# A graph network on one core: attention heads in TensorE's columns, and layer 2's edges in chunks of 128 as they lie

## The chip, the cores and the metric

The kernel runs on one core of one Trainium2 chip, as one program. The metric is the time of one execution on the device in microseconds (us); the median of ten runs is given. TensorE is PE in the profile, VectorE is DVE, ScalarE is ACT, GpSimd is POOL, SyncE is SP; PEld is TensorE's loading of weights.

## What is computed

Four layers act on 3125 nodes of 256 features and 100,000 edges, sorted by their target. Each layer is a graph part, a mixing part and a mixture of experts. The change touches the graph parts of layer 2 and layer 3. In short:

```python
# layer 2: the edges' messages, some of them dropped, summed at the target
h = x @ W_pruned.T
norm = |h[src]| * |edge_weight|            # compared with a tenth of its mean
keep = (norm >= 0.1 * mean) | locked[dst] | (src == dst)
agg = segment_sum(edge_weight * keep * h[src], dst)
x = x + agg + b                            # the mixing part is added too

# layer 3: graph attention with 4 heads of 64 features; each node has an edge to itself as well
e = leaky_relu(a_src[src] + a_dst[dst], 0.2)
a = softmax of e over the edges into each dst
x = x + relu(sum over edges of a * h[src])
```

`locked` marks the nodes that a list of 1000 node numbers names.

## The kernel before

**Names.** P = 125 nodes make a block and there are NB = 25 blocks; PIECES are 7 pieces of 500 nodes (the last has 125). `self.x` holds the nodes' features, `self.xt` the normalised features turned (features in partitions). `self.bank()` hands out one of four PSUM banks named `ps`. `evac` copies out of PSUM on DVE and ACT in turn. `arrive(i)` counts the parts that have finished for a piece and starts the norm of the next step when all are there; `together` runs two generators side by side, each yielding the share of it that is done.

**How the order comes about.** The program is written as straight Python; when it is built, each engine gets a fixed order of its instructions. The semaphores between the engines are added then. Nothing is reordered while it runs.

**Preparation** (`prep`). The edges are packed into records of two words (target x 4096 + source, weight) and stored in DRAM as `rec_d`, in the order of the input. `ROOM[b]` is the number of chunks of 128 edges that is reserved for block b; they sum to NC2 = 841. `idx2` holds where each block's edges start.

**Layer 1's experts** (`l1_ffn`). Eight experts run one after the other over 7 pieces: two matmuls with an activation on ACT (L1411, L1416), then one whose result DVE adds into `self.x` (L1422). Layer 2's preparation `l2_prepare` is a generator that is advanced twice from here, once ahead of expert 0 and once after expert 1. Its first part gathers the records by 25 indirect DMAs (`rec_b`, L1445), a block's chunks beside one another. Its second part finds the locked nodes (L1464), spreads them over 128 partitions as `lock` (25 matmuls L1471, copies L1473), and takes the records apart into `idx` (source), `rel` (target less the block's first node), `wgt`, `awt` and `same`.

**Layer 2's graph part** (`l2_gnn`). A head computes column norms (14 squares with sums, L1503), prunes the weights, and writes h with its norm to DRAM as `hx_d`. Then, block by block and in groups of up to 8 chunks: one gather for each chunk of 128 edges (`hg`, L1551, on POOL); `keep` (L1555, L1556); then for each chunk DVE builds a matrix of edges by the block's nodes (L1560), multiplies it by the larger of `lock` and `keep` (L1562), and PE adds its product with `hg` to the block's sum (L1564). Layer 2's mixing part runs beside it.

**Layer 3's graph part** (`l3_gnn_mix`, `l3_dense`). Attention is computed densely: a matrix of edge counts `ctt_d` (sources by targets) lies in DRAM. For two pieces of targets at a time (1000 columns, four groups in all), the targets' factors `rows` are made by matmuls with a repeated column (L1878) and exponentials (L1880). Then for two heads at a time and each block of sources: `cs` is loaded on SP's queue, ACT makes `t5` (L1899), DVE makes `z` (L1902), and PE multiplies `xr`, the sources' 64 features and a column of ones, with `z` into one PSUM bank for each head and piece (L1905). The 65th row of each result is the sum by which the others are divided. After 25 blocks the banks are copied out, turned by transposes (L1920, L1929) and finished on DVE. Layer 3's mixing part runs beside it.

Of the kernel before, what the change touches and what calls it, by code (L numbers as in the profile page):

```python
# [12 lines left out]
F32 = mybir.dt.float32  # L13
I32 = mybir.dt.int32
# [3 lines left out]
AF = mybir.ActivationFunctionType  # L18
OP = mybir.AluOpType
AX = mybir.AxisListType  # L20
PSUM = bass.MemoryType.PSUM
# [45 lines left out]
ROOM = [_room(b * P, b * P + P) for b in range(NB)]  # L67
NC2 = sum(ROOM)

# [19 lines left out]
class Net:  # L89
    NE, TS = 16, 384  # L90

    def __init__(self, tc, a, ctx):
# [14 lines left out]
        self.iota_f = c.tile([128, 128], F32, name="iota_f")  # L107
        nc.gpsimd.iota(self.iota_f, pattern=[[1, 128]], base=0, channel_multiplier=0,
# [171 lines left out]
    def prep(self):  # L280

        nc, a = self.nc, self.a
        self.rec_d = self.dram.tile([1, 2 * EP], F32, name="rec_d")
# [3 lines left out]
        self.idx2 = self.c.tile([128, NB], I32, name="idx2")  # L287
        nc.vector.memset(self.viol, 0.0)
        nc.scalar.dma_start(self.tab, nc.inline_tensor(_tables(), name="windows").ap())
        room = np.stack([np.broadcast_to(np.array(ROOM) * 128.0, (128, NB)),  # L290
                         np.arange(128)[:, None] * 2.0 * np.array(ROOM)], 1).astype(np.float32)
        with ExitStack() as s:
# [3 lines left out]
            nc.scalar.dma_start(rm, nc.inline_tensor(room, name="room").ap())  # L296
# [72 lines left out]
            nc.vector.tensor_sub(gap2, sr[:, 1:], sr[:, :NB])  # L369
            nc.vector.tensor_tensor(gap2, gap2, rm[:, 0, :], op=OP.is_gt)  # L370
            nc.vector.tensor_reduce(self.viol[:, 2:3], gap2, axis=AX.X, op=OP.add)
            i2 = sb.tile([128, NB], F32, name="i2")
            nc.vector.scalar_tensor_tensor(i2, sr[:, :NB], 2.0, rm[:, 1, :], op0=OP.mult, op1=OP.add)
            nc.vector.tensor_scalar(self.idx2, i2, float(2 * EP - 1024), None, op0=OP.min)
# [983 lines left out]
    def l1_ffn(self, before, after):  # L1358
# [4 lines left out]
        with ExitStack() as s:  # L1363
# [25 lines left out]
            def last(i, w):  # L1389
                self.norm_turn_piece(i, w)  # L1390

                x = self.x[:, i // P:(i + w) // P]
                nc.vector.tensor_add(x, x, self.e2["bias"][:P, None, :].to_broadcast([P, w // P, D]))

# [37 lines left out]
    def l2_prepare(self, sb, wk):  # L1432
# [4 lines left out]
        e["w"] = self.load_w(sb, "L2_gnn_W")  # L1437
        li = wk.tile([P, LOCKS // P], I32, name="li", bufs=1)
# [3 lines left out]
        rec = wk.tile([128, NC2, 2], F32, name="rec_b", bufs=1)  # L1442
        c0 = np.cumsum([0] + ROOM).tolist()
        for b in range(NB):
            nc.gpsimd.indirect_dma_start(  # L1445
                out=rec[:, c0[b]:c0[b + 1]].rearrange("p c t -> p (c t)"), out_offset=None, in_=self.rec_d,
                in_offset=bass.IndirectOffsetOnAxis(ap=self.idx2[:, b:b + 1], axis=1))
# [17 lines left out]
        locked = sb.tile([P, NB], F32, name="locked")  # L1465
        nc.vector.tensor_scalar(locked, ps[:P, :NB], 0.0, None, op0=OP.is_gt)

        lock = sb.tile([128, NB, P], F32, name="lock")
# [5 lines left out]
        pk = rec.bitcast(I32)[:, :, 0]  # L1474
        idx = sb.tile([128, NC2], I32, name="idx")
        rel = sb.tile([128, NC2], F32, name="rel_b")
        nc.vector.tensor_scalar(idx, pk, 4095, None, op0=OP.bitwise_and)
        nc.vector.tensor_scalar(idx, idx, N - 1, None, op0=OP.min)
        dI = wk.tile([128, NC2], I32, name="dI", bufs=1)
        nc.vector.tensor_scalar(dI, pk, 12, None, op0=OP.arith_shift_right)  # L1480
        same = sb.tile([128, NC2], F32, name="same")
        nc.vector.tensor_tensor(same, idx, dI, op=OP.is_equal)
        for b in range(NB):
            nc.vector.tensor_scalar(rel[:, c0[b]:c0[b + 1]], dI[:, c0[b]:c0[b + 1]], float(-P * b), None, op0=OP.add)
        wgt = sb.tile([128, NC2], F32, name="wgt")
        nc.vector.tensor_copy(wgt, rec[:, :, 1])
        awt = sb.tile([128, NC2], F32, name="awt")
        nc.vector.scalar_tensor_tensor(awt, wgt, -1.0, wgt, op0=OP.mult, op1=OP.max)
        e.update(lock=lock, idx=idx, rel=rel, same=same, wgt=wgt, awt=awt, c0=c0)
        yield  # L1490

    def l2_gnn(self, sb, wk, pa):
        nc, tc, a = self.nc, self.tc, self.a
        hx = self.dram.tile([N, D + 1], F32, name="hx_d")
        w, lock, idx, rel, same, wgt, awt, c0 = (
            self.e2[k] for k in ("w", "lock", "idx", "rel", "same", "wgt", "awt", "c0"))

        ss = sb.tile([128, HB], F32, name="ss")
        sp = sb.tile([128, HB, len(PIECES)], F32, name="sp")
        for k, (i, n) in enumerate(PIECES):  # L1500
            for h in range(HB):
                sq = wk.tile([128, PW], F32, name="sq", bufs=1)
                nc.scalar.activation(sq[:, :n], self.xt[:, h, i:i + n], AF.Square, accum_out=sp[:, h, k:k + 1])  # L1503
# [41 lines left out]
        for b in range(NB):  # L1545
            ps = pa.tile([P, D], F32, name="acc")
            for c in range(c0[b], c0[b + 1], CPG):
                m = min(CPG, c0[b + 1] - c)
                hg = wk.tile([128, CPG, D + 1], F32, name="hg", bufs=4)
                for j in range(m):  # L1550
                    nc.gpsimd.indirect_dma_start(  # L1551
                        out=hg[:, j, :], out_offset=None, in_=hx,
                        in_offset=bass.IndirectOffsetOnAxis(ap=idx[:, c + j:c + j + 1], axis=0))
                keep = wk.tile([128, CPG], F32, name="keep")
                nc.vector.tensor_mul(keep[:, :m], hg[:, :m, D], awt[:, c:c + m])  # L1555
                nc.vector.scalar_tensor_tensor(keep[:, :m], keep[:, :m], lim, same[:, c:c + m],  # L1556
                                               op0=OP.is_ge, op1=OP.max)
                for j in range(m):
                    to = wk.tile([128, P], F32, name="to", bufs=16)
                    nc.vector.tensor_scalar(to, self.iota_f[:, :P], rel[:, c + j:c + j + 1],  # L1560
                                            wgt[:, c + j:c + j + 1], op0=OP.is_equal, op1=OP.mult)
                    nc.vector.scalar_tensor_tensor(to, lock[:, b, :], keep[:, j:j + 1], to,  # L1562
                                                   op0=OP.max, op1=OP.mult)
                    nc.tensor.matmul(ps, to, hg[:, j, :D], start=(c + j == c0[b]), stop=(c + j == c0[b + 1] - 1))  # L1564
                yield 0.05 + 0.95 * (c + m) / NC2
            nc.vector.tensor_add(self.x[:, b, :], self.x[:, b, :], ps)
            if b % 4 == 3 or b == NB - 1:
                self.arrive(b // 4 * PW)

    def l2_gnn_mix(self):  # L1570
        with ExitStack() as s:
            ms = s.enter_context(self.pool("m2_sb"))
            mw = s.enter_context(self.pool("m2_wk", 2))
            sb = s.enter_context(self.pool("g2_sb"))
            wk = s.enter_context(self.pool("g2_wk", 2))
            pa = s.enter_context(self.pool("g2_ps", 2, space=PSUM))
            mix = self.l2_mix_by_pieces(ms, mw)
            next(mix)
            self.expect(2, self.norm_turn_mean)
            self.together([self.l2_gnn(sb, wk, pa), mix])  # L1580
# [201 lines left out]
    def l3_gnn_mix(self, before, arrivals):  # L1782
# [6 lines left out]
        with ExitStack() as s:  # L1789
# [12 lines left out]
            xr = sb.tile([P, NB, 4, 65], F32, name="xr")  # L1802
            nc.gpsimd.memset(xr[:, :, :, 64:65], 1.0)
            al = sb.tile([P, NB, 8], F32, name="al")
            for b in range(NB):
                ps = self.bank()
                self.mm_tok(ps[:P, :264], self.xt, b, wx)
                nc.vector.tensor_copy(xr[:, b, :, :64], ps[:P, :D].rearrange("p (h d) -> p h d", h=4))
# [22 lines left out]

            us = sb.tile([P, 3, NB, 4], F32, name="us")
# [5 lines left out]
            self.together([self.l3_dense(sb, wk, pa, wx, xr, us, bias), mix], (1.0, 1.15))  # L1838
# [11 lines left out]
    def l3_dense(self, sb, wk, pa, wx, xr, us, bias):  # L1850
# [5 lines left out]
        at = free[:65, 8 * PW:12 * PW].rearrange("p (h d) -> p h d", h=2)  # L1856

        def finish(b, h0, nh, acc):

            nc.vector.tensor_scalar(few[:, b, h0:h0 + nh], acc[:, :, 64], 1e-20, None, op0=OP.is_lt)  # L1860
            rd = wk.tile([P, 4], F32, name="rd")
            nc.vector.tensor_scalar(rd[:, :nh], acc[:, :, 64], 1e-20, None, op0=OP.max)
            nc.vector.reciprocal(rd[:, :nh], rd[:, :nh])
            t = wk.tile([P, 4, 64], F32, name="tf")
            nc.vector.tensor_mul(t[:, :nh], acc[:, :, :64], rd[:, :nh, None].to_broadcast([P, nh, 64]))
            v = self.x[:, b, h0 * 64:(h0 + nh) * 64]
            nc.vector.scalar_tensor_tensor(v, t[:, :nh].rearrange("p h d -> p (h d)"), 0.0, v,
                                           op0=OP.max, op1=OP.add)

        done, there = 0, []  # L1870
        for p0 in range(0, len(PIECES), 2):
            pcs = PIECES[p0:p0 + 2]
            n = sum(w for _, w in pcs)
            for h in range(4):
                for k, (i, w) in enumerate(pcs):
                    ps = self.bank()
                    for c in range(HB):
                        nc.tensor.matmul(ps[:P, :w], wx[:, c, 260 + h:261 + h].to_broadcast([128, P]),  # L1878
                                         self.xt[:, c, i:i + w], start=(c == 0), stop=(c == HB - 1))
# [478 lines left out]
```

## Time and profile before

| | us |
|---|---|
| median of 10 runs | 4825.16 (4818.94 to 4833.33) |
| the profiled execution's own time | 4822.59 |
| its span, first to last instruction | 4820.8 |
| PE busy | 3788.2 (79% of the span) |
| DVE busy | 2452.4 (51%) |
| ACT busy | 1322.5 (27%) |
| POOL busy | 1122.2 (23%) |
| mean granted TensorE clock | 0.86 |
| layer 1's experts 2 to 7 | 1830 to 2233 |
| head of layer 2's graph part | 2233 to 2275 |
| layer 2's edges, first gather to last | 2275.7 to 3356.0 |
| layer 3's dense attention, first `t5` to last matmul | 3644.4 to 4549.5 |

A line of a group gives the source line, the engine and the operation, what it writes and reads, shapes and count, then the busy time, the mean length of one in ns, and the idle time of the engine just before such instructions with what ended it. Busy times count overlapping instructions once. A matmul of float32 operands shows as two records of PE, each with a weight load of its own. In a line of the timeline the first number is the start, the second the length, both in us; what stands in brackets is the engine's idle time before it and what ended that.

### The profile page before, as it was taken

To read this page: it belongs to the slowest core of one execution; us is meant where nothing else is said; L and a number is where in the kernel's file an instruction comes from. 1 tells how busy PE (TensorE), PEld (TensorE's weight loads), DVE (VectorE), ACT (ScalarE), POOL (GpSimd) and SP (SyncE) were. 2 spreads that over 40 slices of the span, in tenths; PEclk is the share of its full clock that TensorE was granted. 3 is DMA by queue.
4 is the path that set the end of the run, shared out by engine and by line. 5 is a ranking of instruction groups with operands and counts; after the bars stand their busy time and mean duration, and the time that the engine had idled before them with its cause. 6 is when DMAs were issued, how large, how long until landed. Compare 5 with 4: busy or idle time off the path is not lost. (4 is left out here: it accounts for less than half of the span.)

```text
span 4820.8 us, 49604 instructions
## 1 busy us (share of the span) xinstructions
PE 3788.2 (79%) x16425; PEld 2514.3 (52%) x16425; DVE 2452.4 (51%) x7872; ACT 1322.5 (27%) x2364; POOL 1122.2 (23%) x1124
## 2 busy tenths in 40 slices
PE   1886895799748799998565556665699999999798
PEld 0675894466534556555444444444464444444465
DVE  6886335454476421115444444555265666667544
ACT  1476100111123223333000000000155655466521
POOL 2000002200143100000777777776000000000011
PEclk8686996799868699999777777777799999999699
DMA  6245611433231000001333333334201112111232
GB/s 179 63 118 139 145 34 37 128 119 118 82 81 25 25 7 14 14 7 44 101 103 104 103 103 103 104 101 116 88 7 37 49 47 55 44 47 52 59 121 65
DMA packets 256290, 360.32 MB, mean 75 GB/s; under 512 B 62959, under 2 KB 199096, under 8 KB 256027
## 3 DMA queue, kind: packets, MB, share of 16 engines
q1 hardware_dynamic: 132514, 168.96, 12.1%
q0 software_dynamic: 66480, 135.56, 10.5%
q10 hardware_dynamic: 57033, 52.54, 3.9%
q8 instruction: 135, 2.21, 0.2%
q14 instruction: 128, 1.05, 0.1%
HBM read 270.31 MB, written 94.92 MB: 76 GB/s over the span
## 5 line engine op out<-in xcount | busy, mean ns | idle before, releaser
L1564 PE MATMUL acc<-hg,to 128*125 128x256 f32 x1682 | 587.4, 516 | 422.3 <-DVE to L1562 399.7
L1551 POOL DMA_INDIRECT hg<-hx_d,idx x841 | 825.2, 981 | 298.1 <-issue 250.0
L1564 PEld LDWEIGHTS acc<-hg,to 128*125 128x125 f32 x1682 | 430.5, 265 | 565.9 <-DVE to L1562 472.8
L1905 PE MATMUL acc<-z,xr 125*65 125x500 f32 (+1 forms) x1400 | 575.0, 553 | 10.4 <-DVE z L1902 8.8
L1902 DVE SCALAR_TENSOR_TENSOR z<-t,us,cs 125x1000 f32<-125x1000 f32 (+1 forms) x400 | 410.1, 1029 | 136.6 <-PE acc L1905 102.9
L1899 ACT ACTIVATE t<-xn,us 125x1000 f32<-125x1000 f32 (+1 forms) x400 | 409.4, 1037 | 237.6 <-DVE z L1902 233.0
L1905 PEld LDWEIGHTS acc<-z,xr 125*65 125x65 f32 x1400 | 188.3, 144 | 313.6 <-issue 269.6
L1422 DVE SCALAR_TENSOR_TENSOR x<-ps,lg,x 125x256 f32<-125x256 f32 x200 | 93.8, 483 | 412.2 <-PE ps L233 412.2
L1555 DVE TENSOR_TENSOR keep<-hg,awt 128x8 f32<-128x8 f32 (+6 forms) x117 | 19.4, 166 | 549.7 <-DMA hg<-hx_d,idx 424.2
L239 PE MATMUL ps<-xt,w 128*128 128x500 f32 (+1 forms) x672 | 270.3, 549 | 9.0 <-DVE x L1422 7.2
L1560 DVE TENSOR_SCALAR to<-iota_f,rel_b,wgt 128x125 f32<-128x125 f32 x841 | 270.6, 362 | 1.3 <-PE acc L1564 0.6
L1562 DVE SCALAR_TENSOR_TENSOR to<-lock,keep,to 128x125 f32<-128x125 f32 x841 | 252.1, 343 | 0.0
L2188 POOL DMA_INDIRECT bx_d<-row,slot x25 | 31.4, 1256 | 925.5 <-ACT t L1899 809.3
L571 PE MATMUL ps<-y,cb 125*125 125x256 bf16 x1875 | 215.5, 280 | 0.0
L571 PEld LDWEIGHTS <-cb 125*125 125x125 bf16 x1875 | 214.3, 141 | 0.1
L779 ACT ACTIVATE k<-k 125x128 f32<-125x128 f32 x50 | 15.8, 315 | 720.5 <-DVE k L778 677.6
L168 ACT ACTIVATE rstd_t<-rstd_t 125x4 f32<-125x4 f32 (+2 forms) x86 | 17.3, 204 | 671.7 <-DVE rstd_t L167 560.9
L233 PE MATMUL ps<-wo,h 128*125 128x256 f32 x800 | 187.7, 386 | 3.6 <-ACT h L1416 2.6
L239 PEld LDWEIGHTS ps<-xt,w 128*128 128x128 f32 x672 | 123.3, 194 | 122.8 <-issue 109.0
L239 PE MATMUL ps<-h,w 128*128 128x500 f32 (+1 forms) x448 | 178.2, 540 | 1.3 <-ACT h L1411 1.3
L239 PE MATMUL pl<-xbt,w 128*128 128x384 f32 x416 | 172.1, 563 | 8.2 <-DVE xbt L1135 5.8
L233 PEld LDWEIGHTS ps<-wo,h 128*125 128x125 f32 x800 | 142.7, 187 | 66.1 <-ACT h L1416 43.7
(558 smaller groups left out, 6288.5 us busy)
## 6 DMA issues: line engine op xcount, KB each, us to landing
cs<-ctt_d SPq DMA_DIRECT2D x150, 218.8 KB
w<-in_L_ffn_w_dram SPq DMA_DIRECT2D x52, 512.0 KB
cnt_d<-cd SPq DMA_DIRECT2D x25, 683.6 KB
cb<-cnt_d SPq DMA_DIRECT2D x25, 683.6 KB
ctt_d<-ct ACTq DMA_DIRECT2D x6, 2734.4 KB
hg<-hx_d,idx POOLq DMA_INDIRECT x841, 2.8
b0x_d<-zero SPq DMA_DIRECT2D x1, 9984.0 KB
xb<-b0x_d SPq DMA_DIRECT2D x26, 384.0 KB
```

What stands on the lines that cost most here:

```text
L233: self.nc.tensor.matmul(ps, xt[:, h, b * P:(b + 1) * P], w[:, h, :], start=(h == 0), stop=(h == k - 1))
L239: self.nc.tensor.matmul(ps, w[:, h, :], xt[:, h, i:i + n], start=(h == 0), stop=(h == k - 1))
L571: nc.tensor.matmul(ps[:P, :D], cf[k][:, h * P:(h + 1) * P], y3[:, b0 + k, j, :], start=(k == 0 and j == 0), stop=(k == m - 1 and j == 2))
L1422: nc.vector.scalar_tensor_tensor(self.x[:, b, :], ps[:P, :D], g[:, b, e:e + 1], self.x[:, b, :], op0=OP.mult, op1=OP.add)
L1551: nc.gpsimd.indirect_dma_start(out=hg[:, j, :], out_offset=None, in_=hx, in_offset=bass.IndirectOffsetOnAxis(ap=idx[:, c + j:c + j + 1], a ...
L1560: nc.vector.tensor_scalar(to, self.iota_f[:, :P], rel[:, c + j:c + j + 1], wgt[:, c + j:c + j + 1], op0=OP.is_equal, op1=OP.mult)
L1562: nc.vector.scalar_tensor_tensor(to, lock[:, b, :], keep[:, j:j + 1], to, op0=OP.max, op1=OP.mult)
L1564: nc.tensor.matmul(ps, to, hg[:, j, :D], start=(c + j == c0[b]), stop=(c + j == c0[b + 1] - 1))
L1899: nc.scalar.activation(t[:, :n], rows[:, k4, :n], AF.Relu, bias=us[:, 2, b, k4:k4 + 1], scale=us[:, 0, b, k4:k4 + 1])
L1902: nc.vector.scalar_tensor_tensor(z[:, :n], t[:, :n], us[:, 1, b, k4:k4 + 1], c, op0=OP.add, op1=OP.mult)
L1905: nc.tensor.matmul(acc[h, k][:, :w], xr[:, b, k4, :], z[:, k * PW:k * PW + w], start=(b == 0), stop=(b == NB - 1))
L2188: st = nc.gpsimd.indirect_dma_start(out=bx, out_offset=bass.IndirectOffsetOnAxis(ap=slot[:, j:j + 1], axis=0), in_=row[:, j, :], in_offset ...
```

## The change

Two edits are made at once.

**Layer 2's edges.** The chunks are no longer reserved block by block: chunk c is edges 128c to 128c + 127 as they lie in the input, 782 in all. `_spans` says at build time which block, or which two blocks, a chunk can fall into (239 of the 782 have two); a deviation from it sets a flag that leads to the general path. `idx2` and the 25 gathers of `rec_b` go; the records are loaded by two plain DMAs with 128 edges along a partition, taken apart, and turned by 21 transposes. The look-up whether an edge's target is locked moves out of the edge loop into `l2_prepare`: for each chunk one DVE operation with an accumulator writes a column of `lk`. In the edge loop the weight is folded into `kw` for a group of 8 chunks, so that one DVE operation makes the matrix (125 or 250 columns), and PE adds it to one block's sum or to two. The squares of the head move to where a piece of `xt` is finished, in layer 1.

**Layer 3's heads.** `xr` loses its column of ones. The matmuls of two heads go to columns 0 to 63 and 64 to 127 of TensorE (`tile_position`) and write one bank; the sums come from further matmuls with 32 columns of ones, each to 32 columns of TensorE, into a third bank. The targets' factors are computed once from `al`, written to DRAM (`r_d`) and loaded spread over the partitions by `target_rows`. `finish` works on 128 rows at a time.

```diff
-ROOM = [_room(b * P, b * P + P) for b in range(NB)]
-NC2 = sum(ROOM)
+NC2 = -(-E // 128)
+def _starts():
+    q = np.sqrt(np.arange(NB) * P / N)
+    return E * q, 4.5 * np.sqrt(E * q * (1 - q)) + 2
+def _spans():
+    at, off = _starts()
+    out = []
+    for c in range(NC2):
+        bs = [b for b in range(NB) if at[b] - off[b] < 128 * c + 128
+              and (b == NB - 1 or at[b + 1] + off[b + 1] > 128 * c)]
+        out.append((bs[0], len(bs)))
+    return out
...
 def l2_prepare(self, sb, wk):
...
-        for b in range(NB):
-            nc.gpsimd.indirect_dma_start(
-                out=rec[:, c0[b]:c0[b + 1]].rearrange("p c t -> p (c t)"), out_offset=None, in_=self.rec_d,
-                in_offset=bass.IndirectOffsetOnAxis(ap=self.idx2[:, b:b + 1], axis=1))
+        nt = -(-NC2 // 128)
+        rec = wk.tile([128, nt, 128, 2], F32, name="rec_b", bufs=1)
+        nc.gpsimd.memset(rec[:, nt - 1], 0.0)
+        flat = self.as_come_d[:, :2 * 128 * NC2].rearrange("o (c t) -> (o c) t", t=256)
+        m = NC2 - 128 * (nt - 1)
+        nc.sync.dma_start(rec[:, :nt - 1].rearrange("p k e t -> p k (e t)"),
+                          flat[:128 * (nt - 1)].rearrange("(k p) t -> p k t", p=128))
+        nc.sync.dma_start(rec[:m, nt - 1].rearrange("p e t -> p (e t)"), flat[128 * (nt - 1):])
         yield
...
+        for out, op, k in ((fr, OP.bitwise_and, 4095), (to, OP.arith_shift_right, 12), (wgt, None, None)):
+            if op is not None:
+                nc.vector.tensor_scalar(part, pk, k, None, op0=op)
+                nc.vector.tensor_copy(whole, part)
+            for t0 in range(0, nt, 4):
+                ps = self.bank()
+                n = min(NC2 - 128 * t0, 512)
+                for t in range(t0, min(nt, t0 + 4)):
+                    nc.tensor.transpose(ps[:, (t - t0) * 128:(t - t0 + 1) * 128],
+                                        rec[:, t, :, 1] if op is None else whole[:, t], self.ident)
+                nc.vector.tensor_copy(out[:, 128 * t0:128 * t0 + n], ps[:, :n])
...
+        lk = sb.tile([128, NC2], F32, name="lk")
+        for c, (b, m) in enumerate(SPANS):
+            junk = wk.tile([128, 2 * P], F32, name="junk")
+            nc.vector.scalar_tensor_tensor(junk[:, :m * P], self.iota_w[:, :m * P], rel[:, c:c + 1],
+                                           lock[:, b:b + m].rearrange("p b n -> p (b n)"), op0=OP.is_equal,
+                                           op1=OP.mult, accum_out=lk[:, c:c + 1])
+        nc.vector.tensor_tensor(to, fr, to, op=OP.is_equal)
+        nc.vector.tensor_tensor(lk, lk, to, op=OP.max)
         yield
...
 def l2_gnn(self, sb, wk, pa):
...
+        for c0 in range(0, NC2, CPG):
+            m = min(CPG, NC2 - c0)
+            hg = wk.tile([128, CPG, D + 1], F32, name="hg", bufs=4)
+            for j in range(m):
+                nc.gpsimd.indirect_dma_start(
+                    out=hg[:, j, :], out_offset=None, in_=hx,
+                    in_offset=bass.IndirectOffsetOnAxis(ap=idx[:, c0 + j:c0 + j + 1], axis=0))
+            kw = wk.tile([128, CPG], F32, name="kw")
+            nc.vector.tensor_mul(kw[:, :m], hg[:, :m, D], awt[:, c0:c0 + m])
+            nc.vector.scalar_tensor_tensor(kw[:, :m], kw[:, :m], lim, lk[:, c0:c0 + m], op0=OP.is_ge, op1=OP.max)
+            nc.vector.tensor_mul(kw[:, :m], kw[:, :m], wgt[:, c0:c0 + m])
+            for j in range(m):
+                c = c0 + j
+                b, nb = SPANS[c]
+                to = wk.tile([128, nb * P], F32, name=f"to{nb}", bufs=10 if nb == 1 else 6)
+                nc.vector.tensor_scalar(to, self.iota_w[:, :nb * P], rel[:, c:c + 1], kw[:, j:j + 1],
+                                        op0=OP.is_equal, op1=OP.mult)
+                for k in range(b, b + nb):
+                    if c == first[k]:
+                        acc[k] = pa.tile([P, D], F32, name="acc")
+                    nc.tensor.matmul(acc[k], to[:, (k - b) * P:(k - b + 1) * P], hg[:, j, :D],
+                                     start=(c == first[k]), stop=(c == last[k]))
+                    if c == last[k]:
+                        nc.vector.tensor_add(self.x[:, k, :], self.x[:, k, :], acc.pop(k))
...
 def l3_gnn_mix(self, before, arrivals):
...
+            r = sb.tile([P, 4, NB], F32, name="r3")
+            for h in range(4):
+                nc.scalar.activation(r[:, h], al[:, :, 4 + h], AF.Exp, bias=bias[:, h:h + 1], scale=0.8)
+            ps = self.bank()
+            nc.tensor.transpose(ps[:4 * NB, :P], r.rearrange("p h b -> p (h b)"), self.ident[:P, :P])
+            rt = sb.tile([4 * NB, P], F32, name="rt3")
+            nc.vector.tensor_copy(rt, ps[:4 * NB, :P])
+            r_d = self.dram.tile([4, N], F32, name="r3_d")
+            nc.sync.dma_start(r_d.rearrange("h (b p) -> (h b) p", p=P), rt)
...
 def l3_dense(self, sb, wk, pa, xr, us, r_d):
...
+        def target_rows(g, h0):
+            if g < len(groups):
+                i, n = groups[g][0][0], sum(w for _, w in groups[g])
+                for h in (h0, h0 + 1):
+                    self.move(nc.sync, rows[:P, h, :n], r_d[h, i:i + n].partition_broadcast(P))
...
                 for b in range(NB):
...
-                        z = wk.tile([P, 2 * PW], F32, name="z", bufs=3)
+                        z = zs[h] = wk.tile([P, 2 * PW], F32, name="z", bufs=4)
...
-                            nc.tensor.matmul(acc[h, k][:, :w], xr[:, b, k4, :], z[:, k * PW:k * PW + w],
-                                             start=(b == 0), stop=(b == NB - 1))
+                    for u, (h0, k, w) in enumerate(units):
+                        for j in range(2):
+                            nc.tensor.matmul(acc[u][64 * j:64 * j + 64, :w], xr[:, b, h0 + j, :],
+                                             zs[h0 + j][:, k * PW:k * PW + w], start=(b == 0), stop=(b == NB - 1),
+                                             tile_position=(0, 64 * j))
+                    for u, (h0, k, w) in enumerate(units):
+                        for j in range(2):
+                            q = 32 * (2 * u + j)
+                            nc.tensor.matmul(acc[2][q:q + 32, :w], self.ones[:P, :32],
+                                             zs[h0 + j][:, k * PW:k * PW + w], start=(b == 0), stop=(b == NB - 1),
+                                             tile_position=(0, q))
...
+                for h0 in hs:
+                    target_rows(g + 1, h0)
+                finish(b0, pcs[0][1] // P, hs[0], 2 * len(hs), acc)
```

## Prediction

> **What bounds the kernel now.** I read the busy times by stage first, then the costliest groups, then the order of single instructions at the three places that the change touches. Columns of the first view: stretch in us, its length, busy time of PE, weight loads, DVE, ACT and POOL with instruction counts, the granted clock, DMA share, GB/s.
>
> ```profile
> 1830.00:2233.00 403.00, 399.32 (x1320) 232.69 (x1318) 99.92 (x245) 126.47 (x183) 0.00 (x0) 1.00 0.03 8
> 2275.00:3360.00 1085.00, 653.99 (x2038) 495.28 (x2036) 516.35 (x2066) 17.93 (x64) 825.22 (x841) 0.77 0.38 103
> 3640.00:4550.00 910.00, 881.21 (x2754) 405.54 (x2752) 604.61 (x1295) 535.80 (x666) 30.20 (x24) 0.97 0.17 47
> ```
>
> Three stages matter. In layer 1's experts (experts 2 to 7 are the first row) PE is busy 399 of 403 us, DVE 100. In layer 2's edges PE and DVE are half idle. In layer 3's dense attention PE is busy 97%. The groups say what paces each:
>
> ```profile
> L1564 PE MATMUL acc<-hg,to 128*125 128x256 f32 x1682 | 587.4, 516 | 422.3 <-DVE to L1562 399.7
> L1551 POOL DMA_INDIRECT hg<-hx_d,idx x841 | 825.2, 981 | 298.1 <-issue 250.0
> ...
> L1905 PE MATMUL acc<-z,xr 125*65 125x500 f32 (+1 forms) x1400 | 575.0, 553 | 10.4 <-DVE z L1902 8.8
> ...
> L1560 DVE TENSOR_SCALAR to<-iota_f,rel_b,wgt 128x125 f32<-128x125 f32 x841 | 270.6, 362 | 1.3 <-PE acc L1564 0.6
> L1562 DVE SCALAR_TENSOR_TENSOR to<-lock,keep,to 128x125 f32<-128x125 f32 x841 | 252.1, 343 | 0.0
> ```
>
> In the edge stage PE waits for DVE's `to`, and behind it DVE's first use of a group waits for `hg` (L1555, 549.7 us): POOL runs its 841 gathers with only issue time between them, so the **gathers pace the stage**, one per (825.2 + 250.0) / 841 = 1.278 us. In the dense stage the 1400 records of L1905 are 700 matmuls, each two records one after the other, 575.0 / 1400 = 0.41 us a record.
>
> The last view is the order of instructions around `l2_prepare`:
>
> ```profile
> 1685.36 0.60 DVE L1477 TENSOR_SCALAR idx<-rec_b 128x841 int32<-128x841 int32 x1 [12.90 <-DMA rec_b<-rec_d,idx]
> ...
> 1690.61 1.04 DVE L1488 SCALAR_TENSOR_TENSOR awt<-wgt 128x841 f32<-128x841 f32 x1
> ```
> ```profile
> 1821.02 8.57 PE L1471 MATMUL ps<-ident,locked 125*128 125x125 f32 x50 [0.28 <-DVE locked L1466]
> 1829.42 3.52 PE L239 MATMUL ps<-xt,w 128*128 128x500 f32 x8
> ```
> ```profile
> 2234.88 1.10 DVE L1560 TENSOR_SCALAR to<-iota_f,rel_b,wgt 128x125 f32<-128x125 f32 x4
> 2235.90 0.15 DVE L169 RECIPROCAL ln_rs<-rstd_t 125x1 f32<-125x1 f32 x1
> 2235.97 0.33 DVE L1560 TENSOR_SCALAR to<-iota_f,rel_b,wgt 128x125 f32<-128x125 f32 x1
> 2236.22 0.41 DVE L187 TENSOR_SCALAR xn<-x,ln_mv,ln_rs 125x256 f32<-125x256 f32 x1
> ```
>
> Two things are to be seen. An engine's order prefers what stands earlier in the program: L1560, late in the program, fills DVE's gaps, and the earlier norm (L169, L187) takes the engine whenever it is ready. And what stands earlier goes first though nobody needs it yet: PE runs all 50 records of L1471, whose result is used 460 us later, ahead of expert 2 (L239).
>
> **Layer 2, gathers.** 841 chunks become 782 (100,000 edges by 128, rounded up), so 59 gathers go: 59 x 1.278 = **-75**. Of the 782, 239 cover two blocks by the rule in `_spans`, so PE gets 1021 matmuls for 841: 360 more records at 587.4 / 1682 = 0.349 us, 126 us. I cost them at nothing: the stage has 1085 - 654 = 431 us of idle PE; without that cover they cost 126. DVE loses L1562 (252 us) and its L1560 grows by 239 wide forms; that is off the path while POOL paces, as are the 60 more small ones of `kw` (98 groups of three for 117 of two).
>
> **Layer 2, edge records.** 25 gathers of `rec_b` become two plain loads on SP, ahead of the first expert weights. DVE's 12.9 us wait goes, and with it PE's 7.2 us behind it (L239 waiting for L1422). Against it stand 0 to 4.5 us by which the loads hold up the weights (782 KB at 179 GB/s, the busiest slice of the page); I take 2: **-5**. The 14 Square pairs move into the last expert's pieces, where ACT is idle two thirds of the time (10 us if that cover is gone). The stage head now waits until 2242.34 for the last pair; the last `xt` copy ends at 2237.9 and one pair takes 1.0, so **-3** (0 to -5.2, PE's whole wait there).
>
> **Layer 2, the lock lookup.** This is the large added term. 782 operations with an accumulator (`lk`) are put into `l2_prepare`, between experts 1 and 2. No row has this form; L1562 is nearest, 252.1 / 841 = 0.300 us each back to back. Width adds (1256 - 348) / 875 = 1.04 ns an element by the two shapes of L1902, so a two-block one is 0.430. The accumulator read adds between 0 and the 0.083 of L327's; I take 0.04, since L327's pairs start 0.98 apart at a length of 1.03. So 543 x 0.34 + 239 x 0.47 = 297 us (266 to 331). They need `lock` (copies from 1821.8 on) and, through 21 new transposes and their copies, `rel`; the block starts between 1822 and 1838, say 1830. By the order just shown they stand ahead of expert 2's L1422 on DVE. Queued behind them are the four L1422 of the first piece, and these hold the four `ps` banks, so PE, which began the second piece at 1839.9, stands until 1830 + 297 + 0.5 = 2127: **+288** (249 to 340). The small precedent is DVE's block at 1685 to 1691.6, during which PE stood 7.2 us for L1422.
>
> **Layer 3.** L1878 goes: 112 records, 48.0 us on the bound engine, **-48**; its exponentials (L1880) were on ACT, off the path. 100 narrow transposes of 65 rows become 75 of 128: 17.4 us against 75 x 7.7 / 50 = 11.6 by L1320's row, **-5**. The start now goes through DRAM, a write and a broadcast read at some 2.8 us each (the landing time of `hg`), while PE has the other branch: +2 (0 to 6). The seven later reloads of target rows wait on SP for ACT's last use; `cs` loads are queued behind them, and DVE's `z` waits for those. Three `cs` buffers, 3 x 2 x 1.25 = 7.5 us of DVE work by L1902, cover that; bare it is 2.8 us each, 20 in all. The 21 wider copies out of the accumulators (28 before) and the fewer operations of `finish` lie on DVE and ACT, which PE covers.
>
> Heads: 4 matmuls of 65 columns a source block become 4 of 64 in column pairs plus 4 of 32 columns for the sums, 2800 records for 1400. If nothing runs beside anything, PE's 575 us become 1150: **+575**. If pairs and fours run wholly side by side, 8 record times become 4 + 2: -144. No row of the trace shows two matmuls at once, so both ends stay. I take a middle case that follows from the two records of each matmul: if they start in the order given, only the second record of one column group can stand beside the first of the next, so everything runs two at a time, the fours too, and 2800 records take as long as 1400: 0. Each turn between 64 and 32 columns may lose the overlap of one record, 300 x 0.42 + 50 x 0.23 = 138 us at most; I take half: **+69**. Layer 3 together: +18.
>
> By the Trainium skill (TensorE: Matmul & The Clock Gate, Measured speedup vs the span model) three column tiles ran 2.38 times as fast as one; at 2.38 / 3 of the ideal the 575 us would be an estimated 543, and the whole 4947. Against the change the skill says (TensorEngine Tiling (Array Packing), Key Properties) that a change of tiling mode drains TensorE; no row here shows one, and it would lie in the +69.
>
> **Sum.** -75 - 5 - 3 + 288 + 18 = +223. The profiled execution took 4822.6 (span 4820.8), 2.6 under the median 4825.2. So 4825 + 223 = **5048 us**.
>
> **Rivals.** First, *the lookup fills gaps*: DVE is idle 403 - 100 = 303 us beside experts 2 to 7, and 297 would just fit; L1560's behaviour at 2235 speaks for it, the program place of `lk` against it. It would cost some 10 in place of 288: 4770, faster than before. It decides from the point where the block costs under 288 - 223 = 65 us, which is where more than three quarters of it slip into gaps. Second, *columns run wholly side by side*: -144 in place of +69, 4835; PE's 97% speaks for a full gain, as DVE (605) and ACT (536) lie below the 910 - 144 - 48 - 5 = 713 that would remain; the two-record form speaks against. Both at once: 4557. Third, *the columns do not overlap*, so the change does not do what its name says: +575 in place of +69, 5554, or 5276 with the lookup in gaps; 0.41 us a record for 65 columns, like L239's 128, speaks for it.
>
> **How the numbers follow.** Forecast 0.29; lookup in gaps alone 0.14; full columns alone 0.17; both 0.20; no overlap with the block 0.10, with gaps 0.10. The forecast's own range is 4940 to 5169 (288 by -39 and +52, 69 by 69 either way). For 8 in 10 the range must reach 4557 and 5276: **4535 to 5290**; outside are 5554 and the tails. Since 0.2% (9.7 us) is about what a measurement of this kernel can tell from no change, 4835 lies on the edge: I give 0.07 of its 0.17 to faster, 0.05 to the same, 0.05 to slower. Faster 0.14 + 0.20 + 0.07 = 0.41, same 0.05, slower 0.54.
>
> **What would show it.** Right: a stretch of 297 us after expert 1 with DVE full of `lk` and PE empty; POOL with 782 gathers at 1.28 us; dense PE records of which two lie over each other. Wrong: L1422 between the `lk` operations; PE in the edge stage near full, with POOL waiting for `hg` buffers; a dense stage of 713 or of 1430 us in place of 930.

## The result, and the profile after

The changed kernel takes 5022.46 us (median of 9 runs, 4978.06 to 5027.05), the kernel before 4824.52 (31 runs): a ratio of 1.0401 with a 95% interval of 1.0386 to 1.0416, **slower**. The forecast was 5048. In the profiled execution (5023.48, span 5021.7) the 200.9 us of longer span lie here; each time is read from the first and last instruction of a stage:

| stage | before | after | difference |
|---|---|---|---|
| start to the first gather | 2275.7 | 2504.1 | +228.4 |
| first gather to the end of the last | 1081.3 | 990.4 | -90.9 |
| from there to the first dense matmul | 296.6 | 299.3 | +2.7 |
| dense stage up to its last wide matmul | 821.9 | 823.6 | +1.7 |
| dense stage, last group (125 targets) | 74.3 | 128.4 | +54.1 |
| rest | 271.0 | 275.9 | +4.9 |

The changed kernel's busy times by stretch follow (stretch, length, then PE, weight loads, DVE, ACT and POOL with counts, granted clock, DMA share, GB/s). The rows are the lookup, the rest of the experts with the head, the edges, the wide dense groups, and the last group.

```profile
1830.00:2069.00 239.00, 3.46 (x16) 2.61 (x15) 239.00 (x1541) 0.53 (x1) 0.00 (x0) 0.51 0.00 0
2069.00:2475.00 406.00, 393.77 (x1295) 229.55 (x1295) 107.30 (x271) 132.43 (x209) 0.22 (x2) 0.99 0.03 10
2504.00:3495.00 991.00, 643.37 (x2363) 511.56 (x2362) 337.55 (x1238) 17.27 (x62) 745.30 (x782) 0.81 0.38 104
3794.00:4617.00 823.00, 813.40 (x3522) 291.23 (x3520) 520.35 (x897) 454.02 (x510) 20.98 (x16) 0.99 0.20 55
4617.00:4746.00 129.00, 126.47 (x472) 58.34 (x468) 49.88 (x205) 51.11 (x111) 9.72 (x8) 0.53 0.07 15
```

The first row is the largest part of the loss: DVE busy in all of 239 us, PE in 3.5. The timeline of PE and DVE at its end, and then DVE's groups in it by shape, show what waited for what:

```profile
2069.90 0.48 DVE L1442 SCALAR_TENSOR_TENSOR x<-ps,lg,x 125x256 f32<-125x256 f32 x1
...
2070.43 6.06 PE L260 MATMUL ps<-xt,w 128*128 128x500 f32 x8 [236.97 <-DVE x L1442]
```
```profile
L1530 DVE SCALAR_TENSOR_TENSOR junk<-iota_w,rel_b,lock 128x125 f32<-128x125 f32 x543 | 148.4, 343 | 0.0
L1530 DVE SCALAR_TENSOR_TENSOR junk<-iota_w,rel_b,lock 128x250 f32<-128x250 f32 x239 | 97.3, 471 | 0.0
L1530 DVE DVE_READ_ACCUMULATOR junk<-iota_w,rel_b,lock 128x1 f32 x782 | 61.3, 78 | 0.0
```

PE has stood 236.97 us for one L1442 (expert 2's add; L1422 before), which stands behind the last lookup. A lookup is 343 or 471 ns long, but the next one starts before it has ended: the busy time is 148.4 / 543 = 0.273 and 97.3 / 239 = 0.407 us each, from start to start it is 0.270 and 0.400, and the reads of the accumulator lie inside it.

In the dense stage, a step is one source block for two heads and two pieces. PE's timeline in the middle of the stage, first a step whose two heads alternate, then one in which a head's two pieces stand behind each other:

```profile
4201.04 1.90 PE L1981 MATMUL acc<-z,xr 125*64 125x500 f32 x8
4202.87 1.05 PE L1987 MATMUL acc<-z,ones 125*32 125x500 f32 x8
4203.85 1.05 PE L1981 MATMUL acc<-z,xr 125*64 125x500 f32 x2
```
```profile
4104.29 3.02 PE L1981 MATMUL acc<-z,xr 125*64 125x500 f32 x8
4107.24 1.04 PE L1987 MATMUL acc<-z,ones 125*32 125x500 f32 x6
```

In the kernel before, seven records behind each other look like this:

```profile
4203.47 3.10 PE L1905 MATMUL acc<-z,xr 125*65 125x500 f32 x7
```

From start to start the eight records of the heads take 1.83 us in the first step, the eight of the sums 0.98: 2.81 a step, where eight records one after the other took 8 x 0.419 = 3.35 before. In the trace the two records of a pair start 6 to 14 ns apart, mostly 7, and the four of the sums 6 or 7 ns apart: **columns do run side by side**. In the second step the heads take 2.95. Of the 150 wide steps 97 have all four pairs side by side and 53 do not (the expectations below count 55). Counted from each record's start to the start of PE's next record, the heads take 1.83 and 2.95 us by their medians; a whole step takes 3.01 and 4.61 by the means, together 3.58 against 3.45 before.

The last group is worse. PE's timeline there:

```profile
4624.04 0.40 PE L1987 MATMUL acc<-z,ones 125*32 125x125 f32 x2
4624.37 0.43 PE L1981 MATMUL acc<-z,xr 125*64 125x125 f32 x2
4624.73 0.40 PE L1987 MATMUL acc<-z,ones 125*32 125x125 f32 x2
4625.06 0.64 PE L1981 MATMUL acc<-z,xr 125*64 125x125 f32 x2
4625.63 0.62 PE L1987 MATMUL acc<-z,ones 125*32 125x125 f32 x2
4626.18 0.68 PE L1981 MATMUL acc<-z,xr 125*64 125x125 f32 x2
4626.79 0.62 PE L1987 MATMUL acc<-z,ones 125*32 125x125 f32 x2
```

Each head's matmul is followed by its own sum, so nothing has a partner here and every instruction turns between 64 and 32 columns. A head takes 0.69 us (4624.04 to 4624.73) and from 4625 on 1.16 (4625.63 to 4626.79): the clock has gone to half, and the stretch's mean is 0.53.

### The profile page after: what moved, and what is told of

Read it like the earlier page. It is cut to its first block, busy times and chain, and to the rows that moved or that the text cites. A ratio compares the mean times of both kernels' runs of the same rounds, so it can differ in the third digit from the quotient of the medians.

```text
span 5021.7 us, 52996 instructions
## 1 busy us (share of the span) xinstructions
PE 3855.3 (77%) x18070; PEld 2483.2 (49%) x18070; DVE 2486.9 (50%) x8419; ACT 1296.1 (26%) x2330; POOL 1019.7 (20%) x1040
## 5 line engine op out<-in xcount | busy, mean ns | idle before, releaser
L1594 POOL DMA_INDIRECT hg<-hx_d,idx x782 | 745.3, 953 | 281.6 <-issue 216.1
L1610 PEld LDWEIGHTS acc<-hg,to 128*125 128x125 f32 x2042 | 454.5, 227 | 312.1 <-DVE to L1605 221.6
L1977 DVE SCALAR_TENSOR_TENSOR z<-xn,us,cs 125x1000 f32<-125x1000 f32 (+1 forms) x400 | 404.5, 1027 | 192.9 <-PE acc L1987 108.6
L1974 ACT ACTIVATE xn<-xn,us 125x1000 f32<-125x1000 f32 (+1 forms) x400 | 409.7, 1038 | 284.5 <-DVE z L1977 274.5
L260 PE MATMUL ps<-xt,w 128*128 128x500 f32 (+1 forms) x672 | 271.3, 551 | 238.5 <-DVE x L1442 237.0
L1981 PE MATMUL acc<-z,xr 125*64 125x500 f32 (+1 forms) x1400 | 423.9, 577 | 7.1 <-DVE z L1977 7.1
L1442 DVE SCALAR_TENSOR_TENSOR x<-ps,lg,x 125x256 f32<-125x256 f32 x200 | 93.9, 483 | 403.4 <-PE ps L254 403.4
L1605 DVE TENSOR_SCALAR to<-iota_w,rel_b,kw 128x125 f32<-128x125 f32 (+1 forms) x782 | 245.2, 382 | 36.6 <-PE acc L1610 30.0
L1987 PE MATMUL acc<-z,ones 125*32 125x500 f32 (+1 forms) x1400 | 261.1, 569 | 0.0
L1981 PEld LDWEIGHTS acc<-z,xr 125*64 125x64 f32 x1400 | 118.9, 146 | 256.0 <-issue 178.3
L1530 DVE SCALAR_TENSOR_TENSOR junk<-iota_w,rel_b,lock 128x125 f32<-128x125 f32 (+1 forms) x782 | 242.3, 382 | 0.0
L1431 ACT ACTIVATE h<-ps,bnb,bng 128x500 f32<-128x500 f32 (+1 forms) x112 | 80.5, 723 | 497.8 <-PE ps L260 497.8
```

The costliest lines, as they stand in the source:

```text
L260: self.nc.tensor.matmul(ps, w[:, h, :], xt[:, h, i:i + n], start=(h == 0), stop=(h == k - 1))
L1442: nc.vector.scalar_tensor_tensor(self.x[:, b, :], ps[:P, :D], g[:, b, e:e + 1], self.x[:, b, :], op0=OP.mult, op1=OP.add)
L1530: nc.vector.scalar_tensor_tensor(junk[:, :m * P], self.iota_w[:, :m * P], rel[:, c:c + 1], lock[:, b:b + m].rearrange("p b n -> p (b n)"), ...
L1594: nc.gpsimd.indirect_dma_start(out=hg[:, j, :], out_offset=None, in_=hx, in_offset=bass.IndirectOffsetOnAxis(ap=idx[:, c0 + j:c0 + j + 1], ...
L1605: nc.vector.tensor_scalar(to, self.iota_w[:, :nb * P], rel[:, c:c + 1], kw[:, j:j + 1], op0=OP.is_equal, op1=OP.mult)
L1610: nc.tensor.matmul(acc[k], to[:, (k - b) * P:(k - b + 1) * P], hg[:, j, :D], start=(c == first[k]), stop=(c == last[k]))
```

## The experiments

e1 to e4 and the three runs marked * are single runs. Those marked * come from a later round in which the kernel before took 4957.85 us, against 4824.49 in the round of e1 to e4; the record names the same chip, 8, for both. They are read by their ratio to it and by stages. Their excess lies in the gathers: these follow each other every 1.43 us by the mean, against 1.26 in e3, but every 1.25 by the median in both, so it is a few long intervals (39 over 1.4 us in e5, 8 in e3). What made them long is open.

The measured dense stages are counted from the first dense matmul to the last (896.2 before, 952.0 after). The expectations of e1, e2 and e4 count from the first `t5` (905 and 955).

**Each half alone.** `e1_heads_only` is the kernel before with all edits from `l3_gnn_mix` on, `e2_edges_only` the kernel before with all others.

> Layer 3's edit alone, layer 2 as before. Theory (the two edits add up; in the dense stage the pairs do run side by side, but in 55 of 150 full steps the order sets the two pieces of one head behind each other, and the narrow steps alternate between 64 and 32 columns): the dense stage keeps the 955 us that it has in the changed kernel against 905 before, about 4875 in all (4860 to 4890). Rival (layer 3 is slow only as a consequence of layer 2's edit, by the clock or by what is left over from it): the dense stage falls to 720 to 800 us and the whole to 4640 to 4720.

> Layer 2's edit alone, layer 3 as before. Theory (237 us of PE standing behind the lookup, 90 us shorter edge stage, 8 us off the head, 8 us more ahead of layer 3): 4825 + 237 - 90 - 8 = 4964, with 4955 to 4980, and the dense stage back at 905. Rival (the standing of PE is partly made good later): below 4930.

Measured: 4876.68 with a dense stage of 951.2 (954.0 from the first `t5`), and 4964.37 with 891.5 (900.6). The halves add up (52 + 140 = 192 of 198), and neither is slow because of the other. The rivals fall.

**The lookups spread.** A share of the lookups is issued after each piece of experts 2 to 7.

```diff
+                            if e > 1:
+                                self.upto = ((e - 2) * N + i + w) / ((NE - 2) * N) * NC2
+                                next(later)
...
         for c, (b, m) in enumerate(SPANS):
+            while c >= self.upto:
+                yield
```

> The changed kernel with its 782 lookups handed out over the pieces of experts 2 to 7, in place of all after expert 1; nothing else differs. Theory (the 237 us are DVE's block standing ahead of expert 2's adds; beside the experts DVE has about 300 us idle): PE's wait goes nearly whole, 4785 to 4810 in all, and the last expert still ends about 410 us after expert 1. Rival (DVE's work has to be paid somewhere, since each expert piece leaves DVE 7.8 of 10.45 us and the adds stand behind lookups): a third to a half of it comes back as short waits, 4870 to 4910.

Measured: 4784.55, against 5022.46, at the near end of the theory's range. The window that begins at the same point as the first row above, up to the end of the experts:

```profile
1830.00:2237.00 407.00, 395.71 (x1309) 231.64 (x1308) 337.39 (x1805) 132.44 (x209) 0.22 (x2) 0.99 0.03 10
```

The same lookups are in it (DVE 337 of 407 us busy), and PE is busy 396, as in the kernel before (399 of 403). All 238 us were the place of the lookups, not their work. With layer 3 as before:

> Layer 2's edit alone with the lookups spread over experts 2 to 7; layer 3 as before. Theory (gathers pace the edge stage, 59 fewer and fewer waits for a buffer are worth 90; the head is 9 shorter): 4825 - 90 - 9 + 8 = 4734, a ratio of 0.981, with 0.978 to 0.985. Rival (the spread lookups' waits are paid in layer 1): above 0.988.

Measured: 4723.63, ratio 0.9792 (0.9777 to 0.9807). So layer 2's edit is worth some 2% without the block.

**The order in the dense stage.** Each of a step's eight matmuls but the first is pinned behind the one written before it on PE.

```diff
-                            nc.tensor.matmul(acc[u][64 * j:64 * j + 64, :w], xr[:, b, h0 + j, :],
+                            mm = nc.tensor.matmul(acc[u][64 * j:64 * j + 64, :w], xr[:, b, h0 + j, :],
...
+                            if u or j:
+                                self.tc.keep_in_program_order(mm)
```

> The changed kernel with the eight matmuls of each source block held in the order in which they are written (two heads of a piece, then the other piece, then the four sums); the same instructions. Theory (order decides: a step with the heads alternating takes 2.81 us by its median against 3.79 with a head's two pieces behind each other, 55 such steps, and the 25 narrow steps take 4.5 us where 2 are enough): 55 x 0.95 + 25 x 2.5 = 115 off, and less of the half clock at the end, 4870 to 4910 in all, dense stage 800 to 840. Rival one (the turns between 64 and 32 columns cost it, 0.09 us each, and these stay): only the narrow steps gain, 4950 to 4970. Rival two (holding the order makes PE wait for the second head's z): no gain or slower, 5020 to 5080.

Measured: 4977.39, dense stage 904.9 against 952.0: 45 to 47 off, less than half of what was expected. None of the three ranges holds; the first rival's lies nearest. The last group gave 31 us of some 62 (97 in place of 128), the wide steps 16 of some 52: the heads' median there is 1.83 but the mean 2.26, as good as unchanged (2.32). PE's timeline of a slow step:

```profile
3919.11 1.05 PE L1981 MATMUL acc<-z,xr 125*64 125x500 f32 x2
3920.09 0.70 PE L1945 MATMUL ps<-ident,at 128*125 128x128 f32 x4
3920.63 0.65 PE L1290 MATMUL ps<-va,k_e 125*128 125x129 f32 x4
3921.12 0.60 PE L1945 MATMUL ps<-ident,at 128*125 128x128 f32 x4
3921.65 1.89 PE L1981 MATMUL acc<-z,xr 125*64 125x500 f32 x6
```

In such steps pinning keeps the order but not the company: the first head's matmul stands alone, and other work is put in ahead of its partner. So the head whose z comes last goes first in the next run (`for j in (1, 0)`, the pieces turned round too), and lookups are spread.

> Lookups spread as before, and in the dense stage the order held with the head whose z is made last going first, so that when its matmul can start all the others can. Theory (what is left of the loss after the order is held is that other branches' matmuls are put between the halves of a pair, because the second z is not there yet; then a step takes 3.79 in place of 2.81): 4977 - 238 = 4739 for the two edits known, and some 30 to 40 of 150 steps lose their 0.97 more, 4690 to 4715. Rival (the steps are slow because DVE and ACT deliver z no faster): 4735 to 4745.

Measured*: 4837.34, ratio 0.9757, that is 4707 where the kernel before takes 4824.5; dense stage 870.5, its wide part 771.5 against e4's 807.8. That is inside the theory's range: in 142 of 150 wide steps the heads' records now take 1.7 to 2.1 us. Next, the step's matmuls were put ahead of everything that is ready:

```diff
+                    with self.tc.high_priority():
                         for u, (h0, k, w) in reversed(list(enumerate(units))):
```

> As the one before, and the dense stage's matmuls are put ahead of the other branch's in TensorE's order as soon as they can start, so that nothing stands between the four of a step. Theory (side by side holds only while nothing is put between): all 150 wide steps near 2.81, that is 150 x 2.81 = 422 against 523 with the order held alone, 4739 - 100 = 4640, with 4620 to 4665. Rival (the other branch, layer 3's mixing part, is kept waiting and is left over at the end): the dense matmuls end earlier, but the whole stays at 4690 to 4740. A third: the turns to and from the full array stay as many, 4690 to 4715.

Measured*: 4886.5, ratio 0.9856 (4755 where the kernel before takes 4824.5), slower than without. The wide stretch did shrink, from 771.5 to 758.7, but the mixing part was left over: its matmuls fill PE's timeline after the last wide matmul, and the last group began 54 us after that. This is the rival of the left-over, and more than it asked for (up to 4740).

**The last group alone.** The group of 125 targets goes back to 65 columns a head, the wide ones stay as changed.

```diff
+                        if narrow:
+                            nc.tensor.matmul(acc[h][:, :n], xr[:, b, h, :], z[:, :n], start=(b == 0),
+                                             stop=(b == NB - 1))
...
-                    for u, (h0, k, w) in enumerate(units):
+                    for u, (h0, k, w) in () if narrow else enumerate(units):
```

> The changed kernel with its last group (125 targets) alone put back into the form of before: 65 columns for each head, a column of ones, no column positions, no separate sums; the wide groups as changed. Theory (layer 3's whole loss lies in this group, where the changed kernel takes 128 us from the last wide matmul to the end of the dense stage and the kernel before takes 74; in the wide groups what the columns give is eaten up): 50 to 58 us less than the changed kernel, a dense stage of 895 to 905. Rival (the clock is at half in this stretch and stays there for any form of it): 10 to 25 less.

Measured: 4962.82 (ratio 1.0287, 1.0271 to 1.0302), 59.6 less, a little more than the theory's 50 to 58; dense stage 896.0. The last group's window:

```profile
4615.00:4688.00 73.00, 56.47 (x279) 38.43 (x271) 48.25 (x206) 48.63 (x111) 9.55 (x8) 0.74 0.12 27
```

PE is less busy than in the changed kernel (56 of 73 us against 126 of 129), and its clock is higher, 0.74 against 0.53. By the balance layer 3's whole loss lay here: what the columns cost in the wide groups was paid for by the factors' part, as the next runs show.

**The factors' part, and the best versions.** `e8_rows_only` is the kernel before with L1878's matmuls replaced by the reads from DRAM.

> The kernel before with one part of layer 3's edit alone: the targets' factors computed once and read back from DRAM at the start of each group, in place of the 112 records of L1878; heads and sums as before. Theory (they lie on the bound engine, 48.0 us; the three later reloads wait for the last use and cost a few us each): 4825 - 48 + 10 = 4787, with 4775 to 4800. Rival (at a group's start DVE and ACT set the pace, so the matmuls stood beside other waits): 4805 to 4825.

Measured*: 4926.61, ratio 0.9937; the dense stage 863.6 against 896.2, 33 less. Counted from the first `t5` it is 866.3 against 905.4, 39 less, which is the theory's 48 - 10. The ratio is inside the theory's range (4800 of 4825 is 0.9948) but at its dear end.

> Lookups spread, the wide steps' order held with the head whose z is made last going first, and the last group in the form of before. Theory: layer 2's 0.981, the wide stretch 771 in place of 822 and the last group 74 as before, that is 91 and 50 off: 4825 - 91 - 50 = 4684, a ratio of 0.971, with 0.966 to 0.976. Rival (the last group needs as long as in the other forms, 96): 0.976 or more.

> As the one before, with the wide steps' matmuls put ahead of the other branch's as soon as they can start. Theory (the other branch's matmuls are then left over at the end of the stage, as was seen with the last group in the changed form): the wide stretch some 13 shorter, the whole 20 to 45 longer than without it. Rival (that left-over lay in the last group's own form): 10 to 15 shorter.

> The version with lookups spread and layer 3 as before (0.979), and in layer 3 the targets' factors read back from DRAM, but heads and sums as before, 65 columns for each head: the best version without the columns. Theory (with the order held the columns give 20 us more than this: dense stage 844 with them, 864 in the run that had the factors alone): 4724 - 30 = 4694, a ratio of 0.972 to 0.976 against 0.970 with the columns. Rival (the whole gain in layer 3 is the factors', the columns give nothing even in order): 0.970 or less.

Measured: e9 4678.87, ratio 0.9698 (0.9685 to 0.9711), **the lowest time of all versions, faster than both kernels**. e12 4745.49 (0.983, 0.9815 to 0.9845), 67 slower, more than was expected: the last group of e12 has PE work of the other branch in it. Its window, e9's first:

```profile
4327.00:4399.00 72.00, 56.03 (x275) 38.47 (x271) 48.21 (x206) 47.99 (x109) 9.55 (x8) 0.74 0.12 27
```
```profile
4323.00:4475.00 152.00, 121.12 (x517) 83.56 (x514) 81.47 (x300) 67.41 (x147) 9.56 (x8) 0.78 0.06 13
```

275 records of PE in 72 us became 517 in 152. e14, with no columns at all, takes 4684.52 (0.9715, 0.9702 to 0.9729): between the two expectations, and its interval overlaps e9's. The wide stretches of e9 and of e14:

```profile
3555.00:4327.00 772.00, 743.59 (x3511) 269.75 (x3510) 519.96 (x895) 450.11 (x503) 19.98 (x16) 0.99 0.22 58
```
```profile
3553.00:4337.00 784.00, 771.06 (x2346) 338.99 (x2344) 545.81 (x1056) 461.52 (x516) 20.46 (x16) 1.00 0.21 57
```

As built in the changed kernel the columns make this stretch longer (823.6 against 784), in order they make it shorter (772). In the profiled executions, made on different chips, the columns have 16 us (dense stage 843.7 against 860.0), in the medians 6. That the columns bring anything, even in order, is **not settled**.

## Why the prediction was right, and where it was not

The direction, the cause of the largest part and the total held: +223 was forecast and +201 came in the trace. Part of that closeness is luck: the lookup's wait was put 51 too high and layer 3 some 40 too low.

- **Gathers**, -75 forecast, -91 measured. The 59 gathers are 74 by their median interval of 1.254 us, the same in both. Of the other 17, 12 is that POOL stood less between gathers: 9 intervals over 1.4 us, 7 us in all above the median, in place of 48 with 19. That PE's 360 more records cost nothing held: PE is busy 643 of 991 us.
- **Edge records and squares**, -8 forecast: 228.4 less PE's wait of 237.0 is -8.6.
- **Lookup**, a block of 297 and a wait of 288 forecast, 242.3 (1826.8 to 2069.05) and 237.0 measured. Place and consequence were right; the step that failed is the price of one lookup, 0.34 and 0.47 us where the starts lie 0.270 and 0.400 apart. That the operations are 0.343 and 0.471 long is chance: the price was 0.300, L1562's busy time over its count, and 0.04 for the accumulator. In the trace of before the operation behind an L1562 starts 0.259 us after it, also where it is another L1562; the busy time of the group also counts the tail of each L1562 beside the first operation of another line. So the accumulator adds 0.011 and not 0.04, and 0.041 of the base was overlap. The width's 0.130 held. The rival that they fill gaps is out for this kernel, though e3 shows that they fit beside the experts.
- **L1878**, -48 forecast. Counted from the first dense matmul the stage is 33 shorter in e8, and 31.5 in e14 than in e11 (860.0 and 891.5); but 32 of the 112 records, 13 us, lie ahead of that matmul. Counted from the first `t5` it is 39 and 38 (862.7 against 900.6). Where the other 10 went is open.
- **Heads and sums**, 0 and +69 forecast. Layer 3 up to the last dense matmul was forecast at +18 and came to 2.7 + 1.7 + 54.1 = +58.5. e14 has the factors' part without the columns: from the end of the last gather to the last dense matmul it takes 1159.7 us, the changed kernel 1251.3. So heads, sums and their transposes cost 91.6, where 69 - 5 = 64 was forecast: 40 in the wide groups (823.6 against 783.5) and 52 in the last (128.4 against 76.6). The step that failed reads: "only the second record of one column group can stand beside the first of the next, so everything runs two at a time, the fours too". Where they stand next to each other in PE's order, pairs and fours run side by side but for the turns; the rival said so. In the wide groups it is the order that ate the gain. In 28 of the 53 steps that do not alternate the second z was not done when the first head's matmuls started; in the other 25 it was, and a head's two pieces stood behind each other all the same. With the order held and the last z first the wide stretch falls from 823.6 to 772.0 (e9), 11.5 under e14's. In the last group the order held gives 31 (e4), and the form of before, with its higher clock, some 25 more (97.1 in e4, 71.7 in e9). For that clock the prediction had no term. The rival's 713 us did not come in any version: the best dense stage is 843.7. The turns (see below) and the mixing part's matmuls between the pairs stayed; how the rest divides is open.
- **Turns** between 64 and 32 columns: eight heads' records would be 4 x 0.419 = 1.68 and take 1.83, eight of sums 0.84 and take 0.98, so a turn is 0.15 us at full clock; 300 turns are 45 us, and the half of 138 was too much for these. In the last group they stand between nearly all instructions.
- The **rest** is 4.9 us longer. It was not forecast, and its cause is open.

## What to carry to other kernels

For operations that stand back to back, take the price from start to start: the length is too much, and busy time over count is too much where other lines stand between. An operation that nobody needs for 400 us is not free because its engine is idle on average: ask what stands behind it in that engine's fixed order, and hand it out in shares. Matmuls that are to run side by side in columns need both their inputs ready at the same place in PE's order; look at the built order, and let the one whose input comes last go first. Where a group is short, count the turns between column widths before giving it the form of the long groups.

## What the runs showed of the hardware

PE's clock can stand at half though PE is hardly ever idle: 0.53 in the last group with PE busy 126.47 of 129 us, on short records in 64 and 32 columns, and 0.74 in e13 with 56.47 of 73 in 65 columns. A stretch from the middle of the changed kernel's last group:

```profile
4650.00:4700.00 50.00, 49.54 (x176) 23.20 (x174) 19.36 (x96) 21.06 (x46) 4.87 (x4) 0.50 0.05 8
```

In the column form (the changed kernel, e1, e3, e4, e5) the clock goes to half 5 to 12 us into the last group and stays there to its end; with 65 columns (before, e9, e13, e14) it returns to full several times, and the mean is 0.69 to 0.74. The Trainium skill (TensorE: Matmul & The Clock Gate, Part 1: The HAM clock gate) says that the clock follows how busy TensorE has been, with full speed after a busy window of some 3.4 us. This trace does not agree: after a wait of 1.29 us that ended at 4622.99, PE's records are gapless until 4649, and yet the clock goes to half at 4625.1, where a head goes from 0.69 to 1.16 us, and does not come back. What the gate counts, no run here shows.

Two columns took 1.83 us for what took 3.35, a factor of 1.83, and four 0.98, a factor of 3.4, turns included. The skill's factor for three column tiles is 2.38 (same page, Measured speedup vs the span model), and the measured ones stand to either side of it.
